# Routed experts on one core: block rows loaded in four shares and turned by VectorE, gate and up results in PSUM tiles of their own

## The chip, the cores and the metric

The kernel runs on one core of one Trainium2 chip. The metric is the device time of one launch in microseconds (us); where a profile is read, it is one further execution, taken with the hardware profiler. Engines are named as the profile names them: PE (TensorE, matmuls; PEld is its weight load), DVE (VectorE), ACT (ScalarE), POOL (GpSimd), SP (SyncE). A "q" behind an engine's name is its instruction queue, on which DMA issues, waits and register loads stand.

## The reference, cut to what matters

Four layers follow each other on x of shape (8, 512, 256), 4,096 tokens of 256 fp32 values: a scan layer, a mixture of experts, an attention layer, and the same mixture of experts again. The change touches the routed part of the mixture:

```python
x = hidden_states.reshape(-1, D)                  # 4096 x 256
topk_idx, tw = _route(x, router_w, bias)          # 4 of 16 experts for each token
combine = (one_hot(topk_idx, E) * tw[..., None]).sum(1)
h = einsum('td,edf->etf', x, gate_w)              # F = 256
u = einsum('td,edf->etf', x, up_w)
y = einsum('etf,efd->etd', silu(h) * u, down_w)
routed = einsum('etd,te->td', y, combine)
```

So each of 16,384 pairs of a token and an expert needs three products of 256 x 256, and the four results of a token are added up.

## The kernel before

**Layers and stages.** The kernel builds the four layers one after the other. While the scan or attention layer runs, batch by batch, the router of the mixture behind it sorts token rows: for each of its four experts a token's row is written by an indirect DMA (L723) into `xg`, a DRAM table with a region for each expert. A row has ROW = 272 values: 256 normed features, four weights, four expert numbers, the token's number, and filling. Then comes a routed stage of its own for the mixture (`routed`), once after the scan and once after attention. All 16 experts' weights lie in SBUF (`w_all`) by then.

**Blocks.** A routed stage goes through LIKELY = 136 blocks of 128 rows, each of one expert, 272 in both stages. Which expert and which rows is known only at run time, so the numbers are loaded into registers of the engines (`values`, four blocks at a time, L833 for PE, ACT and DVE, L840 for SP). A run behind a condition (L963) covers blocks above 136 and is not entered with these inputs. For each block:

- `load`: SP issues one DMA of the block's 128 rows, 272 values each, into a tile `rows` of 1,024 columns (L860). Blocks from 2 on take it from nine buffers (tag `kb4`, KB = 9).
- `fetch`: the block's gate weights are copied by ACT and its up weights by DVE out of `w_all` to a fixed place (L875).
- `turn`: PE transposes the 128 x 256 features in two matmuls against the identity into a PSUM tile `pt` (L882), and ACT copies it back into the same `rows` tile (L883).
- `up`: sixteen matmul instructions of 128 columns (L893; an fp32 product is two instructions) give gate and up results in one PSUM tile `ph` of 128 x 512, one bank, four deep (`big=4`). ACT takes the sigmoid of the gate half (L901), DVE multiplies twice (L902, L903) and writes `act` into `rows`. DVE also picks the row's weight for this expert (`gain`, L906 and L914).
- `down`, two blocks later: four matmul instructions of 256 columns (L921), ACT scales by the gain (L929), and POOL issues an indirect DMA that adds the 128 rows to the tokens' rows of `part` in DRAM (L930). Blocks alternate between two `part` tables. A block's `rows` buffer is free again when this scatter-add has landed.

**What sets the order.** `run` writes out, for block n: load n+2, fetch n+1, up n, turn n+1, down n-2. Each engine takes its instructions in one fixed order and waits in place for what the next one needs. That order is made before the launch by a scheduler that places instructions by readiness and free buffers and uses the order of the text as priority; so an engine's order need not be that of the text (at a stage's start ACT does the gate copies of three blocks in a row). `tc.issue_after(x)` places what follows behind x on the same engine; `tc.keep_in_program_order` pins one instruction.

**Work beside the blocks.** In the first routed stage POOL loads sums of `part` for the first batches of the attention layer, DVE norms them; in the second POOL loads finished sums of both `part` tables (L1429), DVE adds them (L1436) and POOL writes the output (L1439).

Of the kernel before, what the change touches and what calls it, by code (L numbers as in the profile page):

```python
# [15 lines left out]
P = 128  # L16
# [44 lines left out]
HELD = 6  # L61

# [14 lines left out]
def tile_hybrid_block(  # L77
# [138 lines left out]
    def load_expert(e: int):  # L216
        at = e * WEXP
        gu = w_all[:, at : at + 2 * KD * F].rearrange("p (s k f) -> p s k f", k=KD, s=2)
        nc.sync.dma_start(out=gu[:, 0], in_=gate_w[e].rearrange("(k p) f -> p k f", p=P))
        nc.sync.dma_start(out=gu[:, 1], in_=up_w[e].rearrange("(k p) f -> p k f", p=P))  # L220
        nc.sync.dma_start(
            out=w_all[:, at + 2 * KD * F : at + WEXP].rearrange("p (k d) -> p k d", k=KF),
            in_=down_w[e].rearrange("(k p) d -> p k d", p=P),
        )
# [598 lines left out]
    def routed(i: int, table, beside):  # L823
# [4 lines left out]
        held = {}  # L828

        def values(n: int):  # L830

            many = min(4, (LIKELY if n < LIKELY else NBLK) - n)
            _, w = nc.values_load_multi_w_load_instructions(  # L833
                weight_at[:, n : n + many],
                engines=[PE, ACT, DVE],
                min_val=0,
                max_val=(E - 1) * WEXP,
                skip_runtime_bounds_check_because="a count of at most E - 1 experts, times WEXP",
            )
            _, r = nc.values_load_multi_w_load_instructions(  # L840
                row_at[:, n : n + many],
                engines=[SP],
                min_val=0,
                max_val=NROW - BLK,
                skip_runtime_bounds_check_because="the blocks table stays within the sorted rows",
            )
            for j in range(many):
                held[n + j] = [w[j], r[j]]

        def load(n: int):  # L850
            if n not in held:
                values(n)
# [7 lines left out]
            nc.sync.dma_start(out=rows[:, 0:ROW], in_=xg[i][bass.ds(held[n][1], BLK), :])  # L860
# [17 lines left out]
        def turn(n: int):  # L878
            rows = held[n][2]
            pt = bank([P, KD, P], f"pt_{i}_{n}", "misc")  # L880
            for k in range(KD):
                nc.tensor.transpose(pt[:, k, :], rows[:, k * P : (k + 1) * P], ident)  # L882
            nc.scalar.copy(rows[:, ROW : ROW + D], pt.rearrange("p k q -> p (k q)"))  # L883

        def up(n: int):
# [3 lines left out]
            ph = bank([P, 2, KF * P], f"ph_{i}_{n}", "big")  # L889
            for s in range(2):  # L890
                for f in range(KF):
                    for k in range(KD):
                        nc.tensor.matmul(  # L893
                            ph[:, s, f * P : (f + 1) * P],
# [6 lines left out]
            nc.scalar.activation(act, ph[:, 0, :], AF.Sigmoid)  # L901
            nc.vector.tensor_mul(act, ph[:, 0, :], act)  # L902
            nc.vector.tensor_mul(act, ph[:, 1, :], act)  # L903

            gain = small.tile([P, TK + 1], FP, tag="gain", name=f"gain_{i}_{n}", bufs=4)
            nc.vector.scalar_tensor_tensor(  # L906
                gain[:, 0:TK],
                rows[:, D + TK : D + 2 * TK],
                expert[:, n : n + 1],
                rows[:, D : D + TK],  # L910
                ALU.is_equal,
                ALU.mult,
            )
# [26 lines left out]
        def run(first: int, last: int):  # L940
            load(first)
            load(first + 1)
            fetch(first)
            turn(first)
            for n in range(first, last + 2):
                if n + 2 < last:
                    load(n + 2)
# [4 lines left out]
                if n + 1 < last:  # L952
                    turn(n + 1)
                if n - 2 >= first:
                    down(n - 2)
                    for work_beside in beside.get(n - 1, ()):
                        work_beside()
# [454 lines left out]
    with banks_of(big=4, misc=2, y=2):  # L1412
# [7 lines left out]
    with banks_of(big=4, misc=2, y=2):  # L1420
# [126 lines left out]
```

## Time and profile before

| | us |
|---|---|
| median of six runs (lowest to highest) | 1728.64 (1725.15 to 1734.28) |
| the profiled execution | 1734.61 |
| its span, from first to last instruction | 1732.9 |
| PE busy in it | 1643.0 (95%) |
| DVE / ACT / POOL busy | 1131.4 / 768.2 / 771.2 |
| first routed stage, first L893 to the end of its last block | 353 to about 745 |
| second routed stage | 1302 to about 1700 |
| matmuls of L893 (gate and up) | 286.6 + 286.2 |
| matmuls of L921 (down) | 280.1 |
| transposes L882 on PE, 544 of them | 103.8 |
| copies of them L883 on ACT, 272 of them | 366 ns each |
| row loads L860, 136 KB each, issue to landing | 2.6 |
| scatter-adds L930, issue to landing | 4.0 |

Busy times of one group are the union of its instructions; matmuls are pipelined, so the mean length of one (some 275 ns for 128 columns) overlaps with its neighbours, and the distance of starts is what a matmul costs PE. DMA issues, semaphores and register loads are not counted as busy.

### The profile page before, as it was taken

How to read it: one execution, taken by the hardware profiler on the slowest of the kernel's cores; microseconds unless marked ns; L12 is line 12 of the kernel's file. 1: busy time of each engine (PE TensorE's matmuls, PEld its weight loads, DVE VectorE, ACT ScalarE, POOL GpSimd, SP SyncE). 2: the span in 40 equal slices, each digit the busy share in tenths (PEclk: the TensorE clock that was granted, in tenths of full speed). 3: DMA queues.
4: the chain of work that ended last, by engine and by line, in shares of the span. 5: the costliest groups of instructions: out<-in, count | busy, mean ns of one | idle time of the engine just before them, and what ended most of it. 6: DMA issues, size and time to landing. Idle time of an engine off the chain costs nothing. (4 is left out here: it accounts for less than half of the span.)

```text
span 1732.9 us, 32460 instructions
## 1 busy us (share of the span) xinstructions
PE 1643.0 (95%) x10448; PEld 1210.6 (70%) x10448; DVE 1131.4 (65%) x3503; ACT 768.2 (44%) x1684; POOL 771.2 (45%) x675
## 2 busy tenths in 40 slices
PE   6899998999999999999999999999999999999993
PEld 3466655589999999954445545544458999989992
DVE  8888877545555655547887787777744755555552
ACT  3223232145555555545454354354215555555551
POOL 3355555535555655430032332332543555455563
PEclk9999999999999999989999999999999999999997
DMA  4444333445556656531022121122534555567666
GB/s 160 145 170 159 138 107 114 160 90 95 95 95 105 110 95 95 101 74 37 13 71 68 64 70 57 64 70 87 187 132 91 96 95 95 108 124 138 121 121 168
DMA packets 149277, 181.36 MB, mean 105 GB/s; under 512 B 16144, under 2 KB 135984, under 8 KB 149104
## 3 DMA queue, kind: packets, MB, share of 16 engines
q0 software_dynamic: 54720, 82.57, 25.8%
q1 hardware_dynamic: 92576, 92.71, 18.0%
q10 hardware_dynamic: 1808, 3.93, 0.6%
q8 instruction: 88, 1.44, 0.3%
q14 instruction: 85, 0.70, 0.1%
HBM read 81.62 MB, written 97.53 MB: 103 GB/s over the span
## 5 line engine op out<-in xcount | busy, mean ns | idle before, releaser
L930 POOL DMA_INDIRECT part<-rows x272 | 425.3, 1564 | 342.6 <-ACT rows L929 244.7
L723 POOL DMA_INDIRECT xg<-sorted_m,slots_m x256 | 259.0, 1012 | 323.8 <-ACT slots_m L720 81.8
L893 PEld LDWEIGHTS ph<-rows,gate 128*128 128x128 f32 x2160 | 283.4, 192 | 15.7 <-ACT rows L883 1.2
L893 PE MATMUL ph<-rows,gate 128*128 128x128 f32 x2160 | 286.6, 276 | 0.6 <-ACT rows L883 0.6
L893 PE MATMUL ph<-rows,up 128*128 128x128 f32 x2160 | 286.2, 276 | 0.0
L921 PE MATMUL pyr<-w_all,rows 128*128 x1088 | 280.1, 380 | 1.1 <-DVE rstd_l L431 1.1
L893 PEld LDWEIGHTS ph<-rows,up 128*128 128x128 f32 x2160 | 264.0, 193 | 0.0
L901 ACT ACTIVATE rows<-ph 128x256 f32<-128x256 f32 x272 | 104.5, 384 | 330.7 <-PE ph L893 330.7
L902 DVE TENSOR_TENSOR rows<-ph,rows 128x256 f32<-128x256 f32 x272 | 115.3, 424 | 191.0 <-ACT rows L901 189.4
L921 PEld LDWEIGHTS pyr<-w_all,rows 128*128 128x128 f32 x1088 | 185.5, 190 | 15.6 <-ACT rows L929 1.5
L875 ACT COPY gate<-w_all 128x512 f32 x270 | 168.8, 627 | 14.2 <-PE ph L893 2.4
L1131 ACT ACTIVATE w_all<-ps_a 128x1024 f32<-128x1024 f32 x128 | 124.4, 1021 | 55.3 <-PE ps_a L1120 52.6
L875 DVE COPY up<-w_all 128x512 f32 x270 | 118.9, 440 | 30.7 <-PE ph L893 17.9
L929 ACT ACTIVATE rows<-pyr,gain 128x256 f32<-128x256 f32 x272 | 128.7, 473 | 15.2 <-PE pyr L921 14.1
L906 DVE SCALAR_TENSOR_TENSOR gain<-rows,expert_b 128x4 f32<-128x4 f32 x272 | 61.1, 225 | 108.9 <-ACT rows L929 82.3
L1120 PE MATMUL ps_a<-w_all 32*128 32x384 f32 (+3 forms) x1024 | 124.9, 485 | 7.4 <-ACT w_all L1131 6.7
L982 PE MATMUL pg_m<-xT_m,su_sb 128*128 128x512 f32 x256 | 125.2, 611 | 0.0
L982 PE MATMUL pg_m<-xT_m,sg_sb 128*128 128x512 f32 x256 | 123.9, 606 | 0.0
L1011 PE MATMUL pd_m<-sd_sb,act_m 128*128 128x256 f32 x512 | 121.2, 382 | 0.3 <-DVE act_m L998 0.2
L903 DVE TENSOR_TENSOR rows<-ph,rows 128x256 f32<-128x256 f32 x272 | 115.0, 423 | 8.4
L1011 PEld LDWEIGHTS pd_m<-sd_sb,act_m 128*128 128x128 f32 x512 | 95.7, 190 | 24.1 <-issue 6.7
L882 PE MATMUL pt<-ident,rows 128*128 128x128 f32 x544 | 103.8, 273 | 6.5 <-DMA rows<-xg 4.9
(223 smaller groups left out, 2138.9 us busy)
## 6 DMA issues: line engine op xcount, KB each, us to landing
rows<-xg SPq DMA_DIRECT2D x272, 136.0 KB, 2.6
part<-x SPq DMA_DIRECT2D x16, 512.0 KB, 3.4
part<-ys_m SPq DMA_DIRECT2D x14, 512.0 KB, 3.1
w_all<-in_L_ffn_gate_w_dram SPq DMA_DIRECT2D x24, 256.0 KB, 5.1
w_all<-in_L_ffn_up_w_dram SPq DMA_DIRECT2D x24, 256.0 KB, 5.6
w_all<-in_L_ffn_down_w_dram SPq DMA_DIRECT2D x24, 256.0 KB, 5.8
sum<-part POOLq DMA_DIRECT2D x10, 512.0 KB, 4.3
xg<-zeros SPq DMA_DIRECT2D x34, 136.0 KB, 2.7
```

The costliest lines, as they stand in the source:

```text
L723: nc.gpsimd.indirect_dma_start(out=xg[i], out_offset=bass.IndirectOffsetOnAxis(ap=slots[:, at : at + 1], axis=0), in_=rows[:, t, :], in_of ...
L875: copy(here, w_all[:, bass.ds(held[n][0] + half * KD * F, KD * F)])
L893: nc.tensor.matmul(ph[:, s, f * P : (f + 1) * P], lhsT=both[s][:, k * F + f * P : k * F + (f + 1) * P], rhs=rows[:, ROW + k * P : ROW + (k ...
L902: nc.vector.tensor_mul(act, ph[:, 0, :], act)
L903: nc.vector.tensor_mul(act, ph[:, 1, :], act)
L921: nc.tensor.matmul(py, lhsT=act[:, f * P : (f + 1) * P], rhs=w_all[:, bass.ds(w + 2 * KD * F + f * D, D)], start=(f == 0), stop=(f == KF - 1),
L929: nc.scalar.mul(rows[:, 0:D], py, gain[:, TK : TK + 1])
L930: nc.gpsimd.indirect_dma_start(out=parts[i][n % 2], out_offset=bass.IndirectOffsetOnAxis(ap=rows[:, D + 2 * TK : D + 2 * TK + 1].bitcast(U ...
L982: made = nc.tensor.matmul(dst, lhsT=w[:, k, f * P : (f + 1) * P], rhs=xnT[:, k, :], start=(k == 0), stop=(k == KD - 1),)
L1011: nc.tensor.matmul(py[:, j, :], lhsT=acts[n][:, f, t * P : (t + 1) * P], rhs=shared[n][3][:, f, :], start=(n == 0 and f == 0), stop=(n == ...
L1120: nc.tensor.matmul(ps[j // 2][:, j % 2, col : col + n], lhsT=k_sb[w][r, o, c * P : (c + 1) * P], rhs=q_sb[r, o, c * P : T], start=True, st ...
L1131: nc.scalar.activation(es[two], ps[two][:, :, 0:cols], AF.Exp, scale=ATT_SCALE)
```

## The change

- `load` of a block takes five DMAs for one. Four on SP each fill 32 partitions with the 256 features: share a holds features 64a to 64a+63 of all 128 rows, laid out so that partition s of the share holds rows s, 32+s, 64+s, 96+s. The fifth, on ACT's queue, loads the 16 further values (weights, expert numbers, token) for all 128 partitions.
- `turn` becomes one transpose on DVE, which turns squares of 32 x 32; with the layout of the shares the result is the full transpose. Feature 2q+k comes to partition q of half k, so gate and up weights are loaded with the same split of their rows, `(p k)` for `(k p)`. There is no PSUM tile and no ACT copy.
- The first two blocks of a run (`heads`) keep the single load and the transposes on PE.
- Loads are written out four blocks ahead (`AHEAD`), turns two ahead. Row numbers are loaded into registers apart from the weights' places, eight at a time, on SP and ACT (`places`).
- On DVE the first product of block n is placed behind the transpose of block n+1, and the gain behind the second product.
- Gate and up results lie in two PSUM tiles of 128 x 256, two deep each, for one of 128 x 512, four deep.

```diff
@@ -59,6 +59,7 @@
 PACE = 2
 SENT = 4
 HELD = 6
+AHEAD = 4
 
 
 SUMMED = {0: DONE[0], 1: 76, 2: 88, 3: 110, 4: 127}
@@ -216,8 +217,8 @@
     def load_expert(e: int):
         at = e * WEXP
         gu = w_all[:, at : at + 2 * KD * F].rearrange("p (s k f) -> p s k f", k=KD, s=2)
-        nc.sync.dma_start(out=gu[:, 0], in_=gate_w[e].rearrange("(k p) f -> p k f", p=P))
-        nc.sync.dma_start(out=gu[:, 1], in_=up_w[e].rearrange("(k p) f -> p k f", p=P))
+        nc.sync.dma_start(out=gu[:, 0], in_=gate_w[e].rearrange("(p k) f -> p k f", p=P))
+        nc.sync.dma_start(out=gu[:, 1], in_=up_w[e].rearrange("(p k) f -> p k f", p=P))
         nc.sync.dma_start(
             out=w_all[:, at + 2 * KD * F : at + WEXP].rearrange("p (k d) -> p k d", k=KF),
             in_=down_w[e].rearrange("(k p) d -> p k d", p=P),
@@ -825,7 +826,7 @@
         weight_at, row_at, expert, many, _ = table
         ACT, DVE = mybir.EngineType.Activation, mybir.EngineType.DVE
         PE, SP = mybir.EngineType.PE, mybir.EngineType.SP
-        held = {}
+        held, heads, known, turns = {}, set(), set(), {}
 
         def values(n: int):
 
@@ -837,19 +838,26 @@
                 max_val=(E - 1) * WEXP,
                 skip_runtime_bounds_check_because="a count of at most E - 1 experts, times WEXP",
             )
+            for j in range(many):
+                held[n + j].insert(0, w[j])
+                known.add(n + j)
+
+        def places(n: int):
+
+            many = min(8, (LIKELY if n < LIKELY else NBLK) - n)
             _, r = nc.values_load_multi_w_load_instructions(
                 row_at[:, n : n + many],
-                engines=[SP],
+                engines=[SP, ACT],
                 min_val=0,
                 max_val=NROW - BLK,
                 skip_runtime_bounds_check_because="the blocks table stays within the sorted rows",
             )
             for j in range(many):
-                held[n + j] = [w[j], r[j]]
+                held[n + j] = [r[j]]
 
         def load(n: int):
             if n not in held:
-                values(n)
+                places(n)
             if n < 2:
 
 
@@ -857,7 +865,17 @@
                 rows = rows.rearrange("p t c -> p (t c)")[:, 0 : 4 * D]
             else:
                 rows = work.tile([P, 4 * D], FP, tag="kb4", name=f"rows_{i}_{n}", bufs=KB)
-            nc.sync.dma_start(out=rows[:, 0:ROW], in_=xg[i][bass.ds(held[n][1], BLK), :])
+            block = bass.ds(held[n][-1], BLK)
+            if n in heads:
+                nc.sync.dma_start(out=rows[:, 0:ROW], in_=xg[i][block, :])
+            else:
+
+                for a in range(QUAD):
+                    nc.sync.dma_start(
+                        out=rows[a * SQ : (a + 1) * SQ, 0:D].rearrange("s (b c) -> s b c", b=QUAD),
+                        in_=xg[i][block, a * KD * SQ : (a + 1) * KD * SQ].rearrange("(b s) c -> s b c", s=SQ),
+                    )
+                nc.scalar.dma_start(out=rows[:, D:ROW], in_=xg[i][block, D:ROW])
             held[n].append(rows)
 
         def fetch(n: int):
@@ -877,40 +895,50 @@
 
         def turn(n: int):
             rows = held[n][2]
-            pt = bank([P, KD, P], f"pt_{i}_{n}", "misc")
-            for k in range(KD):
-                nc.tensor.transpose(pt[:, k, :], rows[:, k * P : (k + 1) * P], ident)
-            nc.scalar.copy(rows[:, ROW : ROW + D], pt.rearrange("p k q -> p (k q)"))
+            xT = rows[:, ROW : ROW + D]
+            if n in heads:
+                pt = bank([P, KD, P], f"pt_{i}_{n}", "misc")
+                for k in range(KD):
+                    nc.tensor.transpose(pt[:, k, :], rows[:, 0:D].rearrange("p (q k) -> p k q", k=KD)[:, k], ident)
+                nc.scalar.copy(xT, pt.rearrange("p k q -> p (k q)"))
+            else:
+
+                turns[n] = nc.vector.transpose(
+                    xT.rearrange("p (k b s) -> p k b s", k=KD, b=QUAD),
+                    rows[:, 0:D].rearrange("p (b i k) -> p k b i", b=QUAD, k=KD),
+                )
 
         def up(n: int):
             _, _, rows, *both = held[n]
 
 
-            ph = bank([P, 2, KF * P], f"ph_{i}_{n}", "big")
+            ph = [bank([P, KF * P], f"ph_{i}_{n}_{s}", f"big{s}") for s in range(2)]
             for s in range(2):
                 for f in range(KF):
                     for k in range(KD):
                         nc.tensor.matmul(
-                            ph[:, s, f * P : (f + 1) * P],
+                            ph[s][:, f * P : (f + 1) * P],
                             lhsT=both[s][:, k * F + f * P : k * F + (f + 1) * P],
                             rhs=rows[:, ROW + k * P : ROW + (k + 1) * P],
                             start=(k == 0),
                             stop=(k == KD - 1),
                         )
             act = rows[:, ROW + D : ROW + D + F]
-            nc.scalar.activation(act, ph[:, 0, :], AF.Sigmoid)
-            nc.vector.tensor_mul(act, ph[:, 0, :], act)
-            nc.vector.tensor_mul(act, ph[:, 1, :], act)
+            nc.scalar.activation(act, ph[0], AF.Sigmoid)
+            with tc.issue_after(turns.pop(n + 1).ins) if n + 1 in turns else nullcontext():
+                nc.vector.tensor_mul(act, ph[0], act)
+            made = nc.vector.tensor_mul(act, ph[1], act)
 
             gain = small.tile([P, TK + 1], FP, tag="gain", name=f"gain_{i}_{n}", bufs=4)
-            nc.vector.scalar_tensor_tensor(
-                gain[:, 0:TK],
-                rows[:, D + TK : D + 2 * TK],
-                expert[:, n : n + 1],
-                rows[:, D : D + TK],
-                ALU.is_equal,
-                ALU.mult,
-            )
+            with tc.issue_after(made.ins):
+                nc.vector.scalar_tensor_tensor(
+                    gain[:, 0:TK],
+                    rows[:, D + TK : D + 2 * TK],
+                    expert[:, n : n + 1],
+                    rows[:, D : D + TK],
+                    ALU.is_equal,
+                    ALU.mult,
+                )
             nc.vector.tensor_reduce(gain[:, TK : TK + 1], gain[:, 0:TK], AX.X, ALU.add)
             held[n][3:] = [act, gain]
 
@@ -938,19 +966,31 @@
             )
 
         def run(first: int, last: int):
-            load(first)
-            load(first + 1)
+            heads.update((first, first + 1))
+            coming = iter(range(first, last))
+
+            def load_to(n: int):
+                for m in coming:
+                    load(m)
+                    if m >= n:
+                        break
+
+            load_to(first + AHEAD - 1)
+            values(first)
             fetch(first)
             turn(first)
             for n in range(first, last + 2):
-                if n + 2 < last:
-                    load(n + 2)
+                load_to(n + AHEAD)
+                if n + 2 < last and n + 2 not in known:
+                    values(n + 2)
                 if n + 1 < last:
                     fetch(n + 1)
                 if n < last:
                     up(n)
-                if n + 1 < last:
+                if n == first:
                     turn(n + 1)
+                if n + 2 < last:
+                    turn(n + 2)
                 if n - 2 >= first:
                     down(n - 2)
                     for work_beside in beside.get(n - 1, ()):
@@ -1409,7 +1449,7 @@
         table = stretch(Scan())
         wqkv_sb, wo_sb = load_attention_weights()
 
-    with banks_of(big=4, misc=2, y=2):
+    with banks_of(big0=2, big1=2, misc=2, y=2):
         instead["one"] = "misc"
         routed(0, table, {**prepared(0), **prepared(1)})
         del instead["one"]
@@ -1417,7 +1457,7 @@
     with banks_of(one=4, pair=2):
         table = stretch(Attention())
 
-    with banks_of(big=4, misc=2, y=2):
+    with banks_of(big0=2, big1=2, misc=2, y=2):
 
         beside = (nc.gpsimd, nc.gpsimd)
 
```

## Prediction, made before the changed kernel was run

> **What bounds the kernel now.** I read the clock and the 40 slices first, then the stages, then one block in the order of time, then the waits of the queues. The table of windows shows the routed stretches full on PE at full clock (columns: length, PE, PEld, DVE, ACT, POOL busy, clock, DMA share, GB/s):
> ```profile
> 600.00:650.00 50.00, 50.00 (x384) 48.08 (x384) 28.02 (x86) 27.68 (x71) 27.30 (x18) 1.00 0.57 95
> ```
> A full PE can still hide gaps in modelled ends, so I take starts. One block of the timeline:
> ```profile
> 603.13 0.38 PE L882 MATMUL pt<-ident,rows 128*128 128x128 f32 x2
> 603.35 1.03 PE L921 MATMUL pyr<-w_all,rows 128*128 x4
> 604.22 1.05 PE L893 MATMUL ph<-rows,gate 128*128 128x128 f32 x8
> 605.11 1.06 PE L893 MATMUL ph<-rows,up 128*128 128x128 f32 x8
> 606.00 0.38 PE L882 MATMUL pt<-ident,rows 128*128 128x128 f32 x2
> 606.22 1.03 PE L921 MATMUL pyr<-w_all,rows 128*128 x4
> ```
> Start to start: pt 0.22, pyr 0.87, gate 0.89, up 0.89 us; 2.87 us a block. Per 128-column matmul that is 0.11 us in pt, gate and up alike: the stream has no hole, so PE's own work sets the pace. The other engines in the same block:
> ```profile
> 603.33 0.38 ACT L901 ACTIVATE rows<-ph 128x256 f32<-128x256 f32 x1 [1.10 <-PE ph L893]
> 603.62 0.37 ACT L883 COPY rows<-pt 128x256 f32<-128x256 f32 x1
> 603.75 0.42 DVE L902 TENSOR_TENSOR rows<-ph,rows 128x256 f32<-128x256 f32 x1 [0.68 <-ACT rows L901]
> 603.87 0.63 ACT L875 COPY gate<-w_all 128x512 f32 x1
> ...
> 604.42 0.47 ACT L929 ACTIVATE rows<-pyr,gain 128x256 f32<-128x256 f32 x1
> 605.17 1.55 POOL L930 DMA_INDIRECT part<-rows  x1 [1.11 <-ACT rows L929]
> 605.31 0.43 DVE L875 COPY up<-w_all 128x512 f32 x1
> ```
> ACT works 0.38 + 0.37 + 0.63 + 0.47 = 1.85, DVE 1.65 (L902, L903, L906, L914, L875), POOL 1.55 of 2.87 us.
>
> The loads are not free-running. The waits of SP's queue and one stretch of POOL's timeline:
> ```profile
> SPq L860 <- DMA part<-rows: 259.1, 125, 10.9
> ```
> ```profile
> 540.63 1.55 POOL L930 DMA_INDIRECT part<-rows  x1 [1.32 <-ACT rows L929]
> 544.97 0.84 POOL L152 DMA_DIRECT2D x<-part  x1 [2.78 <-DMA part<-rows]
> 546.11 1.58 POOL L930 DMA_INDIRECT part<-rows  x1 [0.30 <-ACT rows L929]
> 552.08 0.91 POOL L151 DMA_DIRECT2D more<-part  x1 [4.39 <-issue]
> 553.29 1.59 POOL L930 DMA_INDIRECT part<-rows  x1 [0.30 <-issue]
> ```
> Nearly every row load (125 of 136) waits until an old scatter-add has landed and freed one of nine buffers. Twice in each such stretch POOL stops for a plain DMA, and scatters back up: from 0.74 us behind L929 to 8.9 us there, and to 12.9, 10.3 and 10.0 us in the second stage.
>
> **PE (the gain).** Blocks 0 and 1 of each stage keep their transposes; 268 of 272 lose two matmuls at 0.11 us: 268 x 0.22 = **-59 us**, pitch 2.65 us. L883 (0.37 us of ACT) goes too, off the path.
>
> **DVE.** One STREAM_TRANSPOSE of 128x256 is added. Nearest rows:
> ```profile
> L1168 DVE STREAM_TRANSPOSE tr_a<-po_a 128x512 f32<-128x512 f32 x32 | 22.7, 711 | 26.1 <-PE po_a L1155 26.1
> L606 DVE STREAM_TRANSPOSE logit_m<-pl_m 128x128 f32<-128x128 f32 x16 | 5.0, 310 | 17.6 <-PE pl_m L595 17.5
> ```
> Between them (711 - 310) / 384 = 1.04 ns a column, so 0.44 us for 256 columns, within 0.31 and 0.71; none reads every second element as this one does, so 0.71 stands as the far end. DVE comes to 2.10 of 2.65 us (2.36 at worst): hidden. In the stretch 550 to 600 us it also does some 5 us of norms per 50: 2.10 + 0.3, still under. The products wait behind the next block's transpose; that one's rows land some 6 us ahead of need (lead below). The cover: down works on the block two iterations back, so the products may slip about 4 us before PE feels it. Queuing the gain behind the products removes a 0.3 us idle of DVE, worth nothing.
>
> The Trainium skill weighs against this step. The rows say 0.31 us for a square on DVE beside 0.11 us on PE. "VectorE: DVE Perf Modes", under its rules for kernel authors, sends a 128x128 transpose to TensorE where PSUM will do, since DVE turns only 32x32 blocks; its 311 ns, given for bf16, agree with the 310 of fp32 here. By the rule the change pays 0.4 us to save 0.22; by the rows it pays on an engine with 1.2 us to spare.
>
> **PSUM.** Depth falls from four blocks to two. Gate of n+2 needs sigmoid (0.38) and the first product (0.42) of n, due about 0.9 us after gate n ends, while it starts 5.3 us after gate n: nothing lost. The sigmoid starts 0.89 us earlier, worth nothing by itself.
>
> **SP and DMA.** SP issues four loads at 0.33 us (L860) where it issued one: 1.33 us a block, and about 0.25 for the register loads (0.92 per four values): fits 2.65, but the last quarter goes out 1.0 us later. A block becomes 512 packets of 256 B and 128 of 64 B for 128 of 1,088 B. The trace's packet records of this queue (medians) are 9 ns for 4 B, 46 for 1 KB, 48 for 1,088 B, 84 for 2 KB, 159 for 4 KB: along that line 18 and 11 ns, so (512 x 18 + 128 x 11) / 16 = 0.66 us per DMA engine for 0.38. Bounds: 0.38 (the same bytes) to 1.92 (each packet as dear as a whole row); I take 0.66, since the 4 B row shows how little a packet costs by itself. The share 0.57 x 2.87 = 1.64 becomes 1.92 us of 2.65; at the far end 3.18, and DMA would be the bound at +83 us. Expert weights in 2 KB pieces: loaded earlier, nothing.
>
> **ACT.** It loses 0.37 and gains a DMA issue (0.36 to 0.47 by the ACT rows of L1429) and register loads (0.31 per four): 1.9 of 2.65. But the issue waits for the same buffer as SP's, and behind it in line stand the sigmoid, the gate copy and L929. PE waits for the gate copy. This is the cost I cannot see: at nothing if the issue comes late enough in ACT's order, a new bound if early (rival below).
>
> **What comes back.** (1) The load of block k goes when the scatter of k-9 lands, 4.2 us after its start, which is three blocks and 2.0 us after that block's transposes. Lead: 6 x 2.87 - 6.2 = 11.0 us now, 6 x 2.65 - 6.2 = 9.7 after. Slack before gate: 11.0 + 1.1 - 2.6 (landing) - 0.6 = 8.9 now (the backlogs above that are where PE waits today), 9.7 + 1.1 - 2.6 - 1.0 - 0.44 = 6.8 after. Four backlogs each lose 2.1 us more, the one of 7.6 us 0.8: 9 us. POOL catches up 0.22 us a block slower, over the some 47 blocks after block 204 that never get clear: 10 us. Together **+20**, from 0 (if backlogs clear) to +35 (if ACT stops with SP). (2) Start: ACT's part of the load of block 3 waits for a buffer freed at 355.04 us, while L883 for blocks 0 and 1 runs at 352.73. If it stands ahead, about 4 us a stage: **+8**, from 0 to 10.
>
> **Sum.** -59 + 20 + 8 = -31. On the profiled execution 1734.6 - 31 = 1704; that execution lies 6 us above the median of the runs, so on the median 1728.6 - 31 = **1698 us**.
>
> **Rivals.**
> Full gain: the backlogs clear and the start costs nothing, -55 to -59: about 1672. For it: POOL has 0.8 us a block left. Against: PE waits on loads already today.
>
> Cover eaten: DVE at 0.71 us, dearer packets or late quarters leave a pitch near 2.80: 268 x 0.07 = -19, with the start -11: about 1718. For it: every engine but PE rises. Against: 0.3 to 0.7 us of room on each.
>
> Slower, by ACT's order: if the issue for block k stands in ACT's line ahead of L929 of k-7 instead of k-6, two blocks must cover L929 to scatter (0.74), scatter to free buffer (4.2), issue (0.37), sigmoid (0.38) and perhaps the copy (0.63): 5.7 to 6.3, so 2.85 to 3.16 us a block, mid 3.0: 268 x 0.13 = +35, with the start +43: about 1772. With three L929 between, 2.1 us: no bound. It decides at one place in the order. For it: gate copies run blocks ahead in the trace, so the order follows readiness, not the text, and real landings are slow. Against: the text puts it behind k-7.
>
> **Chances.** Forecast (1682 to 1715) 0.37, full gain 0.15, cover eaten 0.20, slower 0.28. A measurement of this kernel tells about 0.3% (5 us) from no change. Of "cover eaten" 0.12 lies beyond that, 0.08 within; slower keeps 0.27. Faster 0.64, same 0.09, slower 0.27. Likeliest case alone: 1682 to 1715. Range 1666 to 1752: half of the slower case (0.14) and little below are left out.
>
> **What would show it.** Right: no L882 but for four blocks, a pitch of 2.65 us in even stretches, STREAM_TRANSPOSE near 0.44 us, PE still at 50 of 50 there, new waits of PE near POOL's plain DMAs. Wrong: ACT's queue waiting on part<-rows in every block, a pitch at or above 2.85, DMA share above 0.9, or PE waiting for DVE's transposes.

## The result, and the profile after

The changed kernel took 1736.72 us (median of 25 runs, 1730.66 to 1744.98); the kernel before, run beside it, 1728.91 us (51 runs, 1722.72 to 1737.16). The ratio is 1.0046, 95% interval [1.0034, 1.0058]: slower by half a per cent, where 1698 us and a gain of 1.8% were forecast. The time lies inside the stated range, on the other side of no change. The profiled execution has a span of 1735.7 us for 1732.9.

**What came as forecast.** TensorE's pace in an even stretch of the changed kernel's timeline (start us, length us, engine, line, operation):

```profile
671.63 1.03 PE L949 MATMUL pyr<-w_all,rows 128*128 x4
...
674.28 1.03 PE L949 MATMUL pyr<-w_all,rows 128*128 x4
```

From pyr to pyr it is 2.65 us. So 91 of the first stage's 135 distances are, and 85 of the second's; before, 124 and 119 were 2.87 us.

**What did not.** The other 94 distances ate the gain, and the loss comes late in a stage. Cut into five stretches of 27 distances, where an even pitch gives 71.6 us, the changed kernel's second stage takes 72.0, 72.2, 84.6, 81.7 and 82.1 us; the kernel before took 77.5, 77.4, 77.4, 83.8 and 74.2. In the first stage it is 71.1, 75.0, 83.1, 80.7 and 80.3. So the gain is there at first, for some 54 blocks of the second stage; then it goes and doesn't come back. The table of windows (length, then PE, PEld, DVE, ACT, POOL busy, clock, DMA share, GB/s) no longer has PE full, where the stretch from 600 us had 50 of 50 before:

```profile
600.00:650.00 50.00, 45.64 (x330) 43.03 (x329) 28.43 (x99) 23.37 (x50) 25.19 (x17) 0.97 0.65 89
```

The page's groups name whom PE waits for, and whom that one waits for (busy and mean ns, then idle time before and what ended most of it):

```profile
L919 PE MATMUL ph<-rows,gate 128*128 128x128 f32 x2160 | 294.2, 280 | 45.5 <-DVE rows L906 44.1
...
L906 DVE STREAM_TRANSPOSE rows<-rows 128x256 f32<-128x256 f32 x268 | 118.0, 440 | 90.8 <-DMA rows<-xg 79.5
```

A transpose costs the 0.44 us of the estimate; but PE waits 44 us for transposes, which wait 80 us for their rows. So the rows come late. Before, SP's queue spent 259 us of a stage waiting for old scatters, well ahead of need. Now its largest wait is another (from 350 to 740 us: total, times, longest):

```profile
SPq L874 <- DMA rows<-xg: 55.1, 41, 4.9
```

SP waits for earlier row loads, and for no buffer: it isn't ahead any more. Followed by their semaphores, 38 of the 40 waits over 0.2 us in the first stage, and 38 of 41 in the second, are for a small load that ACT issued. The landings themselves are not slower: a share lands 2.4 us (median) after its issue, where the whole row load took 2.6. The records of SP's queue, first of the changed kernel, then of the kernel before (min/median/max ns), show what it does instead:

```profile
L874 SPq FUSED_REGOPS  x1072: 37/46/51, 341.6 to 1702.2; - x179
L874 SPq MOVE rows<-xg x1072: 29/29/29, 342.1 to 1702.2; - x179
L874 SPq DMA_DIRECT2D rows<-xg x1072: 316/317/1882, 348.2 to 1702.6; - x179
...
L848 SPq TENSOR_LOAD <-lines_b x34: 1663/1784/2882, 336.3 to 1677.0; - x34
```

```profile
L860 SPq DMA_DIRECT2D rows<-xg x272: 332/333/364, 342.2 to 1691.7; - x136
```

The issue itself still takes 0.32 us. But each load has two register instructions in front, and there is time between the records, so inside one block the shares start 0.51 us apart. Adding SP's records up from start to start between 365 and 745 us, waits taken out, gives 0.56 us for each of 512 loads (285 us), 1.84 for each of 15 register loads (28), and 8 for semaphores: 321 us at work, 58 waiting, 380 in all. (Some 19 of the 285 us are the excess of single issue records that last up to 1.88 us; nothing here shows what holds those.) In 1320 to 1700 us it is 315 and 62. A block's four issues and its eighth of a register load come to 4 x 0.56 + 0.23 = 2.47 us, with semaphores 2.5, of 2.65. **SP had become the full engine**: with its waits there is no time left, and SP isn't in the page's table of busy engines.

**Where each microsecond went**, by starts of pyr in both traces. First pyr: 0.8 us later. The stages, first to last pyr: 385.7 to 390.2 and 390.3 to 392.7, where 135 x 2.65 = 357.8 was to be had. Between the stages -0.6, behind the last pyr -4.3 (30.9 to 26.6; the cause is open). Together +2.8, the difference of the spans.

**One stop in the timeline** (ACT, DVE and PE of the changed kernel around 605 us):

```profile
600.88 0.39 ACT L927 ACTIVATE rows<-ph 128x256 f32<-128x256 f32 x1 [0.41 <-PE ph L919]
602.92 0.35 ACTq L878 DMA_DIRECT2D rows<-xg  x1
```

```profile
610.02 0.45 DVE L906 STREAM_TRANSPOSE rows<-rows 128x256 f32<-128x256 f32 x1 [3.35 <-DMA rows<-xg]
```

```profile
606.87 1.03 PE L949 MATMUL pyr<-w_all,rows 128*128 x4
610.62 2.03 PE L919 MATMUL ph<-rows,gate 128*128 128x128 f32 x8 [2.71 <-DVE rows L906]
```

Between the first two lines ACT loads eight row numbers into registers (L848, 1.75 us in its queue), so its small load goes at 602.92. SP's next share waits from 602.4 to 606.4 us for the semaphore that this small load counts up: in this program the loads of SP and ACT share eight completion semaphores in turn, and an issue waits until the load eight places before it has landed. (This one took 3.5 us to land, where the median small load of the stage took 2.3.) With one load a block that was eight blocks back; with five it is less than two. DVE then stands for 3.35 us before it can turn the rows, PE stops for 2.71 us, and runs the next matmuls at half speed (2.03 us for 1.05).

### The profile page after: what moved, and what is told of

Same layout as the page of the kernel before. It is cut to its first block, busy times and chain, and to the rows that moved or that the text cites. A ratio compares the mean times of both kernels' runs of the same rounds, so it can differ in the third digit from the quotient of the medians.

```text
span 1735.7 us, 35522 instructions
## 1 busy us (share of the span) xinstructions
PE 1602.7 (92%) x9912; PEld 1152.6 (66%) x9912; DVE 1183.4 (68%) x3771; ACT 718.7 (41%) x1416; POOL 773.2 (45%) x675
## 5 line engine op out<-in xcount | busy, mean ns | idle before, releaser
L919 PE MATMUL ph<-rows,gate 128*128 128x128 f32 x2160 | 294.2, 280 | 45.5 <-DVE rows L906 44.1
L906 DVE STREAM_TRANSPOSE rows<-rows 128x256 f32<-128x256 f32 x268 | 118.0, 440 | 90.8 <-DMA rows<-xg 79.5
L957 ACT ACTIVATE rows<-pyr,gain 128x256 f32<-128x256 f32 x272 | 128.8, 474 | 87.1 <-PE pyr L949 56.6
L929 DVE TENSOR_TENSOR rows<-ph,rows 128x256 f32<-128x256 f32 x272 | 106.8, 393 | 44.2 <-ACT rows L927 43.7
L930 DVE TENSOR_TENSOR rows<-ph,rows 128x256 f32<-128x256 f32 x272 | 115.0, 423 | 25.4 <-DVE rows L929 1.4
L1160 PEld LDWEIGHTS ps_a<-w_all 32*128 32x128 f32 x1024 | 48.6, 188 | 70.8 <-ACT w_all L1171 27.4
```

What stands on the lines that cost most here:

```text
L906: turns[n] = nc.vector.transpose(xT.rearrange("p (k b s) -> p k b s", k=KD, b=QUAD), rows[:, 0:D].rearrange("p (b i k) -> p k b i", b=QUAD ...
L919: nc.tensor.matmul(ph[s][:, f * P : (f + 1) * P], lhsT=both[s][:, k * F + f * P : k * F + (f + 1) * P], rhs=rows[:, ROW + k * P : ROW + (k ...
L930: made = nc.vector.tensor_mul(act, ph[1], act)
L957: nc.scalar.mul(rows[:, 0:D], py, gain[:, TK : TK + 1])
L1160: nc.tensor.matmul(ps[j // 2][:, j % 2, col : col + n], lhsT=k_sb[w][r, o, c * P : (c + 1) * P], rhs=q_sb[r, o, c * P : T], start=True, st ...
```

## The experiments

Stages are given by their length from first to last pyr in us (before: 385.7 and 390.3; changed: 390.2 and 392.7). Ratios are to the kernel before on the same chip; its median there was 1727.4 us (runs 1 to 4), 1754.8 (5 to 8), 1726.5 (9 to 12) and 1756.7 (13 to 15), so across these groups only ratios and stages compare. A stage is read from one execution, and that is coarse: the first stage of runs 1, 5 and 6 has the instructions of the changed kernel's first stage, PE's and SP's in the same order, and took 385.8, 386.1 and 383.2 us where that took 390.2. A difference of stages below some 7 us is not read as an effect. Two theories stood after the first four runs: **A**, the shared semaphores that ACT's late load holds, and **B**, SP's own time for its issues.

### 1. One load a block in the second stage

```diff
-            if n in heads:
+            if n in heads or i == 1:
                 nc.sync.dma_start(out=rows[:, 0:ROW], in_=xg[i][block, :])
```

In that stage the rows lie in another order than the transpose expects, so the second half of the output is made of other rows; all sizes are kept.

> In the second routed stage alone each block's rows come by one load on SP, as before, and VectorE turns what lies there; the squares are then not in their places, so the products of that stage are of other rows (data, not work, is left out). Changed kernel: 1736.7 us, its second stage 392.7 us from the first to the last L949 block. If the loss sits on the load side (five DMAs a block), the stage falls by 25 to 32 us and the kernel to 1705 to 1712. If VectorE's turn itself is the cause (its place in VectorE's order), the stage keeps its 393 us and the kernel 1737.

1.0143 [1.0125, 1.0161]; stages 385.8 and 406.5. Neither. The scheduler had moved another thing: the transpose of a block now stood four or five blocks ahead of its products (one in the changed kernel), behind loads that couldn't have come. The waits of its second stage, SP's and DVE's:

```profile
SPq L870 <- DMA part<-rows: 297.2, 117, 18.2
```

```profile
DVE rows L906 <- DMA rows<-xg: 133.2, 83, 4.2
```

SP was ahead again; DVE stood 133 us in front of early transposes, with other blocks' products behind them in its line. Run 5 repeats this with the transpose held in its place.

### 2. Only the split of the PSUM tile, in the kernel before

```diff
-            ph = bank([P, 2, KF * P], f"ph_{i}_{n}", "big")
+            ph = [bank([P, KF * P], f"ph_{i}_{n}_{s}", f"big{s}") for s in range(2)]
```

> The kernel before with only the gate and up results in PSUM tiles of their own, two deep each. No theory gives this a price: 1729 us, within 0.3%. A pitch above 2.87 us or new waits of PE for VectorE would say that two tiles are too few.

1.0191 [1.017, 1.0213]; stages 404.7 and 403.0. The split by itself costs 1.9%. The weight loads of its PE wait (second stage):

```profile
PEld ph L893 <- ACT rows L883: 29.9, 87, 0.5
```

With the sigmoid free earlier, the scheduler put the gate copy ahead of the copy of the PE transpose in ACT's order; that copy came 0.3 us late in two of three blocks, and their pitch is 3.08 us. It is order again, not depth.

### 3. All five loads on SP

```diff
-                nc.scalar.dma_start(out=rows[:, D:ROW], in_=xg[i][block, D:ROW])
+                nc.sync.dma_start(out=rows[:, D:ROW], in_=xg[i][block, D:ROW])
```

> The 16 further values of a row come by SP's queue instead of ACT's; ACT also loads no row numbers. Theory A (SP's shares wait in turn for completion counters that ACT's late small load holds): the long waits of SP go, and the kernel is 15 to 35 us faster than the changed one, 1702 to 1722. Theory B (SP has no time left: four issues 0.51 us apart and 1.75 us of register loads per eight blocks): five issues make 2.55 + 0.22 = 2.77 us a block, so no even stretch at 2.65, the pitch is 2.77 or more, and nothing is gained beyond that: about 1715 at best, 1750 if each stop is never made good.

1.0214 [1.0176, 1.0251], 1761.6 us; stages 407.9 and 408.1: B in kind, but beyond its 1715 to 1750 us, since a load costs more than the 0.51 us put in. SP's timeline:

```profile
605.52 1.84 SPq L874 DMA_DIRECT2D rows<-xg  x4
607.55 0.35 SPq L878 DMA_DIRECT2D rows<-xg  x1
608.16 1.84 SPq L874 DMA_DIRECT2D rows<-xg  x4
...
612.84 0.35 SPq L878 DMA_DIRECT2D rows<-xg  x1
615.42 3.16 SPq L874 DMA_DIRECT2D rows<-xg  x4
```

Four shares of 0.35 us take 1.84 us, five loads 2.64 us (605.52 to 608.16), and a register load stands in the hole before 615.42. Summed as above, SP is at work 391 of 395 us in the first stage and waits for no load and no scatter. At 5 x 0.56 + 0.23 = 3.03 us a block, 135 blocks are 409: SP's time sets the stage by itself. This shows that issues on SP can be the bound; in the changed kernel they are one fifth fewer.

### 4. ACT's small load into a place of its own, up to nine blocks ahead

```diff
-                nc.scalar.dma_start(out=rows[:, D:ROW], in_=xg[i][block, D:ROW])
+            tails[n] = b_out_sb[:, n % TAILS * (ROW - D) : (n % TAILS + 1) * (ROW - D)]
+            nc.scalar.dma_start(out=tails[n], in_=xg[i][bass.ds(held[n][-1], BLK), D:ROW])
```

`b_out_sb` lies idle in the stages; with TAILS = 16 places in it, ACT's load needs no `rows` buffer.

> ACT's small load goes into a place of its own (sixteen of them), up to nine blocks ahead, so that it waits for no row buffer. Theory A: it has landed long before SP comes to its counter, PE's waits for VectorE's turn shrink to a third: 1697 to 1717. Theory B: SP has as much to issue as in the changed kernel, the stalls stay: 1730 to 1737. Theory C (small packets crowd the DMA engines and landings are late): stays at 1737 too.

1.0641 [1.0605, 1.0678]; stages 432.3 and 438.7. SP's wait in the first stage:

```profile
SPq L884 <- DMA b_out_sb<-xg: 96.0, 47, 6.1
```

SP's share waits for ACT's load to another tile, with which the program ties it by the semaphore alone. That such waits exist is shown. The 6% isn't all theirs, though: in that stage the work of ACT itself stood some 79 us behind its own loads, which wait in the same turn (56 us) and for old scatters (23 us). From here on A and B are the question.

### 5. One load a block in the second stage, the transpose held in place

```diff
+                with tc.issue_after(made_last[0].ins) if i == 1 and made_last else nullcontext():
                     turns[n] = nc.vector.transpose(
```

on top of run 1 (and the same rows in the wrong place); `made_last` is the second product of two blocks before.

> Theory A (the load shares wait for completion counters that they share with ACT's late small load) and theory B (SP needs about 0.56 us for each share, 2.5 us of each block's 2.65, and can make no stop good) both say that the load side alone costs the gain. In the second stage alone each block is one load on SP again (the row places in it are then another order than VectorE's turning expects, so the second half of the output holds products of wrongly placed rows; every instruction's size is kept), ACT loads nothing, and the turning of a block is held behind the products of two blocks before, where it stands in the changed kernel. A and B: second stage 360 to 372 us instead of 392.7, so the kernel at 1705 to 1718 us, ratio 0.987 to 0.993; PE waiting for VectorE's turned rows under 6 us in that stage instead of 22. Rival (VectorE's turning itself, not the loads, keeps PE waiting): the second stage stays at 388 to 396 us and the kernel at 1733 to 1740 us.

0.9898 [0.9866, 0.993]; stages 386.1 and 373.0 in one execution, where without the edit the second was the longer one. PE's waits in the first, then in the second, and the first stop of the second:

```profile
PE ph L920 <- DVE rows L907: 14.2, 13, 2.2
```

```profile
PE ph L920 <- DVE gain L944: 11.2, 6, 3.7
```

```profile
1568.51 0.45 DVE L907 STREAM_TRANSPOSE rows<-rows 128x256 f32<-128x256 f32 x1 [3.87 <-DMA rows<-xg]
...
1569.10 1.13 PE L920 MATMUL ph<-rows,gate 128*128 128x128 f32 x8 [2.79 <-DVE gain L944]
```

The profile names the gain, but each of the six stops ends 0.6 us behind the start of a transpose that had itself waited 1.2 to 4.9 us for its rows. So late rows are left, 11 us where under 6 were expected, but only behind POOL's backlogs, from 1568 us on. By stretches of 27 distances the stage takes 73.7, 71.5, 71.5, 82.6 and 73.6 us: after the backlogs it comes back to the pitch. 373.0 is 1 us beyond the span expected, 15 above 135 x 2.65: the loads cost the gain, and POOL's backlogs keep a part.

### 6. The same with three further loads on SP

```diff
+                if n not in heads:
+                    for a in range(1, QUAD):
+                        nc.sync.dma_start(
+                            out=rows[a * SQ : (a + 1) * SQ, 784:1024].rearrange("s (b c) -> s b c", b=QUAD),
```

(second stage; rows in the wrong place as in run 5, and the three loads fill columns that nothing reads)

> As the run with one pinned load, with three more loads of a share's size per block on SP in the second stage, which fill columns that nothing reads: four issues per block on SP, none on ACT, so no completion counter is shared with ACT's queue. Theory B (SP's issue time): the second stage is 383 to 395 us, like the changed kernel, 1729 to 1740 us in all. Theory A (the wait for counters that ACT's late load holds): 360 to 375 us, 1705 to 1720 us in all.

0.9977 [0.9945, 1.0009]; stages 383.2 and 382.4: just outside B's span, and between the two theories. Beside the changed kernel's 1.0046 run 5 gains 1.5%, this run 0.7%. So three more issues, with ACT issuing nothing, took back about half of what run 5 had gained. The stretches suggest how: 73.6, 71.5, 74.9, 84.2 and 78.2 us. With four issues a block SP keeps the pitch at first, and behind the backlogs it recovers less than run 5 does. The proof isn't clean, since the DMA share rose too, to 0.76 (0.61 in run 5).

### 7. One of the four shares on ACT

```diff
-                    nc.sync.dma_start(
+                    (nc.scalar if a == QUAD - 1 else nc.sync).dma_start(
```

> The changed kernel with the fourth share of each block issued by ACT instead of SP: SP has 3 issues a block (3 x 0.56 + 0.23 = 1.9 us of 2.65), ACT two instead of one. Theory B: SP has time to catch up, stages 365 to 380 us, 1695 to 1722 us in all. Theory A: two of five loads now stand behind ACT's own work and hold more of the counters, stages 400 us or more, 1750 us or more in all.

1.0903 [1.0836, 1.0971]; stages 457.7 and 458.9. It looked like A, but the orders differ: the transpose stands three to four blocks ahead, much as in run 1, and ACT's loads mostly stand behind the L957 of eight blocks before, not five. Inconclusive by itself; runs 8 and 9 explain it.

### 8. Every second block the old way

```diff
-            heads.update((first, first + 1))
+            heads.update((first, first + 1), range(first + 1, last, 2))
```

> The changed kernel with every second block taken the old way: one load on SP and TensorE's transposes, 2.87 us of TensorE, the other blocks in four shares with VectorE's turning, 2.65 us. Mean pitch without waits 2.76 us, 135 x 2.76 = 372.6 us a stage, and SP at (0.56 + 4 x 0.56) / 2 + 0.23 = 1.6 us a block. Both theories: the shares are issued in time, stages 372 to 382 us against 390.2 and 392.7, so 1700 to 1722 us in all; theory A keeps some of the waits for ACT's late load, at half as many places. If the schedule puts the two kinds of blocks in each other's way (PSUM tiles or VectorE's order), 390 us or more a stage.

1.0736 [1.0671, 1.0802]; stages 435.1 and 457.9. In this kernel too the transpose and ACT's load had moved ahead. One stop of its timeline:

```profile
1511.31 1.87 SPq L874 DMA_DIRECT2D rows<-xg  x4
1511.32 0.38 ACTq L878 DMA_DIRECT2D rows<-xg  x1
...
1511.75 0.38 ACT L927 ACTIVATE rows<-ph 128x256 f32<-128x256 f32 x1 [2.95 <-DMA part<-rows]
```

SP and ACT are let go by the same scatter, and the sigmoid behind ACT's load has been idle for 2.95 us.

### 9. The same, with the transpose held in place

```diff
+                with tc.issue_after(made_last[0].ins) if made_last else nullcontext():
                     turns[n] = nc.vector.transpose(
```

> The run that alternated the two kinds of blocks lost 7% with two things out of place against the changed kernel: VectorE's turning stood four to five blocks ahead of its block's products instead of two, and ACT's small load stood directly behind the L957 of the block whose buffer it takes plus one, so that ACT waits there for POOL's scatter. This kernel puts back only the first (the turning is held behind the products of two blocks before). If VectorE's place was the cause: stages 373 to 390 us, ratio to the kernel before 0.985 to 1.000. If ACT's wait for the scatter is the cause (the prediction's third rival, in another place): stages still 415 us or more, ratio 1.045 or more.

1.0751 [1.0729, 1.0773]; stages 434.3 and 454.8. The transpose's place changed nothing: it is ACT. How long ACT's queue stands before its small load, in the changed kernel and in this one (min/median/max ns):

```profile
L878 ACTq EVENT_SEMAPHORE  x276: 17/38/252, 352.2 to 1699.1; - x138
```

```profile
L878 ACTq EVENT_SEMAPHORE  x142: 17/4313/9149, 353.6 to 1804.1; - x142
```

38 ns where the load mostly stands behind the L957 of five blocks before; 4.3 us where it stands behind that of eight, one block after the buffer's last reader, with the scatter still to land.

### 10. The same, with no load on ACT

```diff
-                nc.scalar.dma_start(out=rows[:, D:ROW], in_=xg[i][block, D:ROW])
+                nc.sync.dma_start(out=rows[:, D:ROW], in_=xg[i][block, D:ROW])
```

> As the run before, and the small load of a turned block is issued by SP, so ACT issues no load and waits for no scatter. SP: (0.56 + 5 x 0.56) / 2 + 0.23 = 1.9 us a block of 2.76. Theory B (SP's room decides): stages 373 to 388 us, ratio 0.985 to 0.998. If it is 400 us or more a stage, neither SP's room nor ACT's wait is what the alternation costs.

0.9956 [0.9931, 0.9982]; stages 374.6 and 386.1, where the pitch alone gives 372.6. Both as B expected.

### 11. Two of three blocks turned by VectorE, all loads on SP

```diff
-            heads.update((first, first + 1), range(first + 1, last, 2))
+            heads.update((first, first + 1), range(first + 1, last, 3))
```

on top of run 10.

> As the run before with two of three blocks turned by VectorE: mean pitch (2 x 2.65 + 2.87) / 3 = 2.72 us, SP at (0.56 + 2 x 5 x 0.56) / 3 + 0.23 = 2.3 us a block. Theory B: some room is left (0.4 us a block), so stages 370 to 390 us, ratio 0.983 to 1.000, and more of SP's waits are paid than with every second block.

0.9915 [0.9899, 0.9932], 1713 us beside 1726: faster than both kernels. Stages 369.1 (expected 370 or more) and 379.9, pitch alone 367.7. The page's group of PE, beside the 45.5 us of the changed kernel:

```profile
L920 PE MATMUL ph<-rows,gate 128*128 128x128 f32 x2160 | 286.3, 276 | 1.2 <-DVE rstd_l L432 0.8
```

PE has next to no idle time in front of gate, and SP waits for buffers again (50 us between 1320 and 1690), so it is ahead.

### 12. The changed kernel without the split of the PSUM tile

```diff
-            ph = [bank([P, KF * P], f"ph_{i}_{n}_{s}", f"big{s}") for s in range(2)]
+            ph = bank([P, 2, KF * P], f"ph_{i}_{n}", "big")
```

> The changed kernel with only the split of the PSUM tile undone: gate and up results in one tile, four deep, as before the change. The prediction held the split to be worth nothing either way; with SP's issues as the bound: the same as the changed kernel within 0.5%, ratio to the kernel before 1.000 to 1.010. If the two-deep tiles keep PE waiting behind a late turning: 0.985 to 0.998. If the earlier sigmoid was worth something here: 1.015 or more.

0.9991 [0.997, 1.0013], between what two of the cases expected; stages 378.6 and 389.9. Against the changed kernel's [1.0034, 1.0058] it is faster by some 0.5%. SP's wait for earlier row loads stays (54 us of its second stage), so I take it that the depth of four only gives PE more to do while the wait lasts.

### 13. Two of three blocks turned, the small load on ACT, held behind the L957 of five blocks before

```diff
+            with tc.issue_after(scaled[-1]) if scaled else nullcontext():
+                nc.scalar.dma_start(out=rows[:, D:ROW], in_=xg[i][block, D:ROW])
```

> Two of three blocks turned by VectorE, SP with four shares for such a block, and ACT issuing the small load where it stands in the changed kernel (held behind the L957 of five blocks before). SP: (0.56 + 2 x 4 x 0.56) / 3 + 0.23 = 1.9 us of 2.72, so SP has room, and ACT's late small load still stands among SP's loads on the completion counters. Theory A (the wait for a counter that ACT's load holds is enough by itself): stages 385 us or more, ratio 1.000 or more. Theory B (the waits are made good where SP has room): stages 370 to 382 us, ratio 0.985 to 0.995.

0.9965 [0.9935, 0.9994]; stages 371.4 and 381.2. By the stages B, by the ratio just beyond its span. SP's first wait is no longer for row loads (390 to 750 us):

```profile
SPq L874 <- DMA part<-rows: 90.2, 60, 5.2
```

ACT's load stands as late as in the changed kernel, and SP all but never waits for it (once, 0.6 us, in the second stage): it does not eat the gain by itself. The ratio lies above run 11's, whose loads all stand on SP, so some cost may be left.

### 14. Run 11 with one PSUM tile, four deep

The diff of run 12, on top of run 11.

> Two of three blocks turned by VectorE with all loads on SP, and gate and up results in one PSUM tile, four deep, as before the change. If the four-deep tile is worth what it gave the changed kernel (0.5%): ratio 0.984 to 0.990. If it only helped to ride out SP's stops: as with the split tiles, 0.989 to 0.994. If the later sigmoid costs here: 0.995 or more.

0.9935 [0.9914, 0.9956]; stages 368.8 and 382.7: as with the split tiles. Where the rows come in time, the split neither costs nor gives.

### 15. Three of four blocks turned, all loads on SP

Run 11 with `range(first + 1, last, 4)`.

> Three of four blocks turned by VectorE with all loads on SP: mean pitch (3 x 2.65 + 2.87) / 4 = 2.705 us, SP at (0.56 + 3 x 5 x 0.56) / 4 + 0.23 = 2.47 us, 0.24 us of room a block where two of three have 0.4 and all blocks have none. Theory B: stages between those of two of three (369.1 and 379.9 us) and those with every block's five loads on SP (407.9 and 408.1), 372 to 392 us, ratio 0.990 to 1.005. If only TensorE's pitch counted: 366.5 and 377 us, ratio 0.988 to 0.991.

0.9869 [0.9825, 0.9913]; stages 370.8 and 378.7, pitch alone 365.2. (The expectation said 366.5 for that; 135 x 2.705 is 365.2.) The best ratio, though its interval meets that of run 11, so which of the two is better stays open. The first stage lies 5.6 us over its pitch where run 11 had 1.4. With 0.24 us of room instead of 0.4, SP may make good a little less, but one trace can't show so small a difference.

**What stands.** The loads cost the gain (run 5). Each of the two suspects leaves a gain where the other is absent: ACT's late load with room on SP (run 13), nearly full SP with no load on ACT (run 15). Together they fill SP's queue. How the 50-odd lost microseconds divide between them isn't settled: run 6 puts about half on SP's time, with more DMA traffic than the changed kernel; and in run 13 the eight places of the semaphores reach 2.2 blocks back instead of 1.6, which may be part of why no wait was left. A kernel with four issues on SP, ACT's load removed and the traffic unchanged was not tried.

## Why the prediction was wrong, step by step

**The step that failed** is SP's: "issues four loads at 0.33 us (L860) where it issued one: 1.33 us a block, and about 0.25 for the register loads (0.92 per four values): fits 2.65". The row was the length of the issue record alone. A load costs SP 0.56 us from start to start; in the kernel before, with one load in 2.87 us, no two stood back to back to show it, though the register instructions of L860 were there to be read. The sum is 2.5 us for 1.6, so the reserve was 0.15 us a block, not 1.1. Beside it fails the step that put ACT's issue "at nothing if the issue comes late enough in ACT's order". It does come late, and a late load on ACT holds SP: that an issue waits for the load eight places before was not in the working at all, and SP waits 58 and 62 us a stage for it, nearly always for ACT's load. The runs show both, and not how the loss divides between them.

**PE, -59.** Right: the pitch is 2.65 us wherever nothing is late, -59.4 us over 270 distances.

**DVE.** Right: 0.44 us, and no product or transpose late by DVE's own work. The Trainium skill's "VectorE: DVE Perf Modes" sends such a transpose to TensorE under its rules for kernel authors; runs 11 and 15, with room on SP, gain with it all the same.

**DMA.** Right: share 0.69 and 0.71 for an estimate of 0.72, and the packets of 256 and 64 B took 18 and 11 ns (median), as drawn from the line. Runs 11 and 15 gain at 0.68 and 0.70 (second stages).

**Backlogs, +20.** The right kind, somewhat smaller. Run 11's stages lie 13.6 us over their pitch, where the kernel before lay 1.1 over its own: 12.5 us, three quarters of it in the second stage. In the changed kernel the stages grew by 66.3 us over the pitch; the 54 beyond I put down to SP's queue, its work and its waits.

**Start, +8.** It was 0.8.

**PSUM, "nothing lost".** Wrong in company: 1.9% by ACT's order in run 2, 0.5% in the changed kernel (run 12), nothing in run 14.

**The third rival, ACT's order.** Not what happened: ACT's queue stands 38 ns before its load. (Its register loads were mis-sized too: 1.96 us for eight values, where 0.31 for four was counted; in the stop shown above one of them stands before the late load.) But the mechanism and its turning point ("at one place in the order") are real: runs 8 and 9 meet it with 4.3 us. I gave it 0.28 and SP none, and looked for the danger in the one queue whose place I could not see, not in the one whose rows I could add up.

**The sum.** -59.4 + 66.3 + 0.8 - 0.6 - 4.3 = +2.8 us, where -59 + 20 + 8 = -31 was forecast.

The signs that I named for a wrong prediction were ACT's queue, the pitch, the DMA share and PE waiting for DVE's transposes. The last one did appear, and the mean distance, 2.89 and 2.91 us, passed the 2.85 named. It was the symptom: the chain leads from it to the rows, and from the rows to SP.

## What to carry to other kernels

Before a load is cut into several, add up the issuing queue as for any engine: start-to-start time of one issue with its register work, times issues, plus register loads, against the pitch; the page's busy table leaves this queue out. A queue with a few per cent of room keeps pace only as long as nothing stops it: at 0.15 us of room a block, a wait of 4 us like the one above takes some 27 blocks to make good (an estimate from these two numbers). And hold every instruction that an experiment doesn't mean to move, because a scheduler that goes by readiness moves transposes, copies and loads along with the edit.

## What the hardware showed unexpectedly

- A dynamically addressed load takes 0.32 us as a record and 0.51 to 0.56 us of SP's time. The Trainium skill's "DMA: Bandwidth & Descriptors", under "Issuing engines are not separate DMA queues", calls the time of initiating a DMA "usually small relative to the DMA itself"; here one took 0.56 us beside 2.4 us to landing, and four of them 2.2 of a block's 2.65 us, so for small loads in a row the measurement decides.
- Loading eight values into registers holds a queue for 1.78 us (SP, median) or 1.96 us (ACT), some 0.22 to 0.25 us a value. ACT's load of four weights' places (L834) took 0.31 us, so the price of a value isn't fixed.
- After a stop of 2.71 us PE ran gate at 2.03 us instead of 1.05, half speed (granted clock 0.61 from 610 to 613 us). Stops so cost more than their length: of the 32.5 us that the changed kernel's first stage lies over its pitch, PE was idle for 24 (383.0 less 358.9 busy, 362 to 745 us), so some 8 were matmuls that took longer, at the lower clock or in starting again.
- ACT's load to one tile can stop SP's load to another (run 4, up to 6.1 us at a time), by the completion semaphore that they share.
